# Attention and a quantised residual block on one core: q's first transfers on three queues, a cast ahead of a square, and a copy into another buffer

## The chip, the cores and the metric

The kernel runs on one core of a Trainium2 chip. The time is device time of one launch in microseconds. The core has five engines with instruction streams of their own: PE (TensorE, matrix products), DVE (VectorE), ACT (ScalarE), POOL (GpSimd) and SP (SyncE, used here only to issue DMA transfers). A transfer is issued by one of SP, ACT and POOL, in the order of that engine's own instructions, and the bytes are moved by DMA engines that all of them use. "PEclk" in the profile is the TensorE clock that was granted, as a share of full speed.

## The reference

Input x has shape (4, 128, 64, 64) in fp32. Two layers follow each other. The first is a group norm, attention with 4 heads of 32 channels over the 4096 positions of each image, a projection, and x added again. The second is a residual block of two 3x3 convolutions with weights quantised to three bits, each with a batch norm over the batch and all positions.

```python
# first layer
xn = group_norm(x)                     # 8 groups of 16 channels
q, k, v = split(einsum('oc,bchw->bohw', qkv_w, xn) + qkv_b)
attn = softmax(einsum('bhid,bhjd->bhij', q, k) * d ** -0.5)
x = x + einsum('oc,bchw->bohw', proj_w, einsum('bhij,bhjd->bhid', attn, v)) + proj_b
# second layer
residual = x
out = relu(batchnorm(conv3x3(x, lsq_quantize(w1)), gamma1, beta1))
out = batchnorm(conv3x3(out, lsq_quantize(w2)), gamma2, beta2)
x = relu(out + residual)
```

## The kernel before

Channels lie on the 128 partitions. The order of all instructions is written by hand: functions emit parts of the work, and a schedule calls them, so each engine executes its instructions in the order in which the Python code emitted them. Where two instructions of different engines touch the same buffer, the framework puts in a wait.

**Attention** takes most of the time. There are 32 blocks (4 images, 8 blocks of 512 queries), each against 32 tiles of 128 keys. `scores` multiplies k by q (L447, tile `s`, the name `s_0_1` below means key tile 0, group 1) and ACT takes the exponential (L449, `p`). `weights` multiplies p by v (L461). Sums of p go to DVE (L476) and to accumulating transfers of POOL. fp32 operands are held as two parts, hi and lo, both in the type fp32r of the matmuls; hi is written by ACT, and lo (the value less hi) by DVE. Projections of later blocks are side work between the scores.

**The start.** Chunks of x are loaded by SP and ACT, statistics and the norm are computed, and `project_parts` makes k, q and v of the first blocks: PE writes `pk`, `pq` and `pv` (L322), `parts` writes hi (L356, ACT) and lo (L357, DVE) into `kst` and `qst`, and these are sent to where the scores read them. For most blocks this goes by DRAM, one transfer of 512 KB out (`kd`, `qd`, L361) and smaller ones back in. For the very first block alone, `direct` (L393 to L409) moves k and q within the on-chip memory: 8 transfers of 64 KB for k (L407), then 8 of 128 KB for q (L409). The first four of each are for g=0 (heads 0 and 1), the next four for g=1 (heads 2 and 3). They go by turns to `nc.sync` and `nc.gpsimd`. SP's next instruction after its four of q is the store `kd` of the second block; POOL's next are two small loads `al`. The scores of a key tile are four matmuls for each g, and the first key tile's g=0 scores read all four transfers of q for g=0.

**The convolutions.** In each layer of the residual block the output is made in 16 bands of 16 rows (1024 positions, two psum banks of 512). Most bands (2 to 14, in the second convolution without 8) are made "by two": two output rows are computed together from sums and differences of input rows, with fewer matmuls. For them `mixed_parts` makes the sums `vo` and `vi` on DVE (L600 to L603), ACT casts them to hi (`uo`, `ui`, L605), and DVE makes lo (`lo`, `li`, L609). `conv_by_two` (L870) issues 24 matmuls into four banks: a0, a1 (inner products), c0, c1 (outer rows). `rows_of_two` then makes the two output rows:

- `copy` (L884, ACT) copies a1 from psum to the odd rows of the result `cv`;
- `inner` (L887 and L889, DVE) writes a0 + a1 to the even rows and a0 − a1 to the odd rows of `cv`, with sums for the batch norm. L889 overwrites in place what L884 wrote and L887 reads;
- `outer` (L894, ACT, twice) copies c0 and c1 into the rows of a buffer `co`, then an accumulating transfer of POOL (L896) adds `co` to `cv`. For bands 13 and 14, `outer_at_once` (L900, DVE) adds c0 and c1 to `cv` directly.

When a band is complete in `cv`, ACT squares it with a running sum (L1011, its output goes to `co` as a place to discard it). This waits for the band's accumulating transfer, so squares are put off: they stand in a list `behind`, and `flush(1)` issues all but the newest. In the loop of `layer`, a band's instructions are emitted in this order: `copy`; in the first convolution `flush(1)`; `begin` (the first part of a later band's preparation: sums and casts); `flush(1)`; `inner`; `rest` (lo of that later band); `later` (loads); `outer`.

Band 15 is the last and is computed in the ordinary way: ACT casts its input tile t to `hi` (L619, in `begin`), DVE makes `lo` (L622, in `rest`), and after the loop PE computes it as `c_last` (L837) in two halves, in banks that band 13's c0 and c1 had before. Batch norm statistics of `c_last` are taken by DVE (L1041), and the batch norm ends the layer.

Of the kernel before, what the change touches and what calls it, by code (L numbers as in the profile page):

```python
# [18 lines left out]
ALU = mybir.AluOpType  # L19
# [8 lines left out]
FB = 512  # L28
# [50 lines left out]
def _fast_body(ctx, tc, x, norm_w, norm_b, qkv_wt, qkv_b, proj_wt, proj_b,  # L79
               w1, alpha1, gamma1, beta1, w2, alpha2, gamma2, beta2, out, cnt):  # L80
    nc = tc.nc
    B, C, H, W = x.shape
# [146 lines left out]
    def stack_tile(name):  # L229
        return kpool.tile([P, KW], F32R, name=name, tag="k")  # L230

    def f32(t):
        return t.bitcast(F32)
# [154 lines left out]
    def k_tile(b, j):  # L388
        ks[b, j] = stack_tile(f"k{b}_{j}")[:, : 2 * FB].rearrange("p (g n) -> p g n", n=FB)
        return ks[b, j]  # L390

    def q_tile(b, j):
        qs[b, j] = qpool.tile([P, 2, 2, FB], F32R, name=f"q{b}_{j}", tag="q")  # L393
        return qs[b, j]

    def direct(what, t):

        u = k_tile(0, 0) if what == "k" else q_tile(0, 0)
        engines = nc.sync, nc.gpsimd
        for g in range(2):  # L400
            for c, s in enumerate((0, 2, 1, 3)):
                i, part = divmod(s, 2)
                h = 2 * g + i
                src = t[h * D : (h + 1) * D, :, :]
                eng = engines[(4 * g + c) % len(engines)]
                if what == "k":
                    eng.dma_start(out=f32(u)[s * D : (s + 1) * D, g, :], in_=src[:, part, :])  # L407
                else:
                    eng.dma_start(out=f32(u)[s * D : (s + 1) * D, g, :, :], in_=src)  # L409
# [420 lines left out]
    def conv(parts, ps, j, w):  # L830
        hi, lo = parts
        r0 = j * RB
        n = 0
        for part in (hi, lo):
            for tap in range(TAPS):
                kh, kw = divmod(tap, 3)
                nc.tensor.matmul(ps.rearrange("p (r w) -> p r w", w=W), w[:, tap, :],  # L837
                                 part[:, r0 + kh : r0 + kh + RB, kw : kw + W],
                                 start=(n == 0), stop=(n == 2 * TAPS - 1))
                n += 1  # L840

    def conv_tile(i, b, g):
        return pss.tile([P, 2, FB], F32, name=f"c{i}_{b}_{g}", tag="s")
# [19 lines left out]
    def conv_by_two(parts, a, c, i):  # L863

        for m, ps, w in ((1, a[0], wmix[:, 0, :, :]), (2, a[1], wmix[:, 1, :, :]),
                         (0, c[0], wq[i][:, 0:3, :]), (3, c[1], wmix[:, 2, :, :])):
            n = 0
            for part in parts:
                for kw in range(3):
                    nc.tensor.matmul(ps.rearrange("p (r w) -> p r w", w=W), w[:, kw, :],  # L870
                                     part[m][:, :, kw : kw + W], start=(n == 0), stop=(n == 5))
                    n += 1

    def rows_of_two(a, c, y, sums, name, at_once):

        def of(t, e):
            return t.rearrange("p (r e w) -> p r e w", e=2, w=W)[:, :, e, :]

        even, odd = of(y, 0), of(y, 1)
        a0, a1, c0, c1 = (u.rearrange("p (r w) -> p r w", w=W) for u in (*a, *c))  # L880
        outer_rows = f32(stack_tile(f"co{name}"))[:, : 2 * FB]

        def copy():
            nc.scalar.copy(odd, a1)  # L884

        def inner():
            nc.vector.scalar_tensor_tensor(even, odd, 1.0, a0, ALU.mult, ALU.add,  # L887
                                           accum_out=sums[:, 0:1])
            nc.vector.scalar_tensor_tensor(odd, odd, -1.0, a0, ALU.mult, ALU.add,  # L889
                                           accum_out=sums[:, 1:2])  # L890

        def outer():
            for e, u in enumerate((c0, c1)):
                nc.scalar.activation(of(outer_rows, e), u, AF.Identity,  # L894
                                     accum_out=sums[:, 2 + e : 3 + e])
            nc.gpsimd.dma_start(out=y, in_=outer_rows, accum_op=ALU.add)  # L896

        def outer_at_once():
            for e, u, v in ((0, even, c0), (1, odd, c1)):
                nc.vector.scalar_tensor_tensor(u, u, 1.0, v, ALU.mult, ALU.add,  # L900
                                               accum_out=sums[:, e : e + 1])

        return copy, inner, outer_at_once if at_once else outer, outer_rows
# [26 lines left out]
    def layer(i, prepare, start=None):  # L930
# [17 lines left out]
        def flush(left=0):  # L948
            while len(behind) > left:
                behind.pop(0)()  # L950

        def stats(m, j, ps):
            if m in on_act:
                return
            nc.vector.bn_stats(st[:, 2 * plain.index(m) + j, :], ps[:, j, :])

        def keep(m, j, ps):
            b, g = bandlist[m]
            c = 2 * g + j
            if m not in on_act:  # L960
                nc.scalar.copy(cv[b][:, c * FB : (c + 1) * FB], ps[:, j, :])
                return
            k = two.index(m)
            nc.scalar.activation(cv[b][:, c * FB : (c + 1) * FB], ps[:, j, :], AF.Identity,
                                 accum_out=sums[:, 4 * k + j : 4 * k + j + 1])
            if j == 1:
                junk = f32(stack_tile(f"co{i}_{m}"))[:, : 2 * FB]
                nc.scalar.activation(junk, cv[b][:, 2 * g * FB : (2 * g + 2) * FB], AF.Square,
                                     bias=shift[:, 1:2], accum_out=squares[:, k : k + 1])

        def origin():
            mv = small.tile([P, 2], F32, name=f"first{i}", tag="mv")
            nc.vector.bn_aggr(mv, st[:, 0:2, :].rearrange("p j s -> p (j s)"))
            nc.vector.tensor_copy(shift[:, 0:1], mv[:, 0:1])
            nc.vector.tensor_scalar(shift[:, 1:2], mv[:, 0:1], -1.0, None, ALU.mult)

        def banks(m):
            b, g = bandlist[m]
            a = conv_tile(i, b, g)
            if (len(two) - 1 - two.index(m)) % 2:  # L980
                c = [psa.tile([P, FB], F32, name=f"c{i}_{b}_{g}{j}", tag="a") for j in "xy"]
            else:
                c = pss.tile([P, 2, FB], F32, name=f"c{i}_{b}_{g}z", tag="s")
                c = [c[:, j, :] for j in range(2)]
            return [a[:, j, :] for j in range(2)], c

        done = start(banks, stats, keep, origin) if start else {}
        for m, (b, g) in enumerate(bandlist[:-1]):
            if m in done and m not in BY_TWO[i]:
                continue  # L990
            begin, rest, later = prepare(m)
            if m in BY_TWO[i]:
                if m in done:
                    a, c = done[m]
                else:
                    a, c = banks(m)
                    conv_by_two(ready[i, b, g], a, c, i)
                y = cv[b][:, 2 * g * FB : (2 * g + 2) * FB]
                k = two.index(m)
                copy, inner, outer, junk = rows_of_two(a, c, y, sums[:, 4 * k : 4 * k + 4], f"{i}_{m}",  # L1000
                                                       m > 12)
                copy()
                if i == 0:
                    flush(1)
                begin()
                flush(1)
                inner()
                rest()
                later()
                outer()  # L1010
                behind.append(lambda y=y, k=k, junk=junk: nc.scalar.activation(  # L1011
                    junk, y, AF.Square, bias=shift[:, 1:2], accum_out=squares[:, k : k + 1]))
                continue
            ps = conv_tile(i, b, g)
            for j in range(2):
                conv(ready[i, b, g], ps[:, j, :], j, wq[i])
            begin()
            flush(1)
            rest()
            later()  # L1020
            for j in range(2):
                stats(m, j, ps)
                keep(m, j, ps)
            if m == 0:
                origin()
# [68 lines left out]
    def opening(banks, stats, keep, origin):  # L1094
# [35 lines left out]
        return {0: None, 1: None, 2: done}  # L1130

    a1, c1 = layer(0, first, opening)
    nc.vector.tensor_copy(cnt, pools["bad"][0:1, 0:1])

# [42 lines left out]
    def second(m):  # L1177
# [10 lines left out]
        return begin, rest, later  # L1188

    a2, c2 = layer(1, second)  # L1190
    for b in (B - 2, B - 1):
        for i in range(4):
# [470 lines left out]
```

## Time and profile before

| what | value |
|---|---|
| time, median of 3 runs | 2470.35 us (2469.05 to 2471.85) |
| profiled execution, its own time | 2469.57 us |
| span of the profiled execution | 2467.9 us |
| mean granted TensorE clock | 0.994 |
| L449 ACT exponentials | 1951.3 us, 2048 of 1033 ns |
| L447 PE scores | 1137.3 us, 8192 |
| L461 PE products with v | 1025.8 us, 16384 |
| L870 PE products by two | 150 for each of uo, ui, lo and li, some 43.9 us each |
| L1011 ACT squares | 28.8 us, 25 of 1152 ns |

The page gives one execution. Each group's first number is its busy time, "xN" the number of instructions, and what follows the bar is how long the engine had stood idle just before them and whom it waited for. Busy time of DVE and ACT is within a tenth of that of PE over the whole, so the page's sums alone do not tell which of them an edit has to reach; the chain of waits and PE's gaps do.

The convolutions lie at the end: the first from about 2250 to 2332 us, the second to 2437, and after it the last additions and stores to 2468. In the table of busy tenths the last slices show it:

```profile
PE   9999999999999999999999999999999999999995
DVE  6899888989998888899989888898999999999897
ACT  5999888999988899999998899999999999996686
DMA  6887677678776766688767676678666666766627
```

### The profile page before, as it was taken

To read this page: it belongs to the slowest core of one execution; us is meant where nothing else is said; L and a number is where in the kernel's file an instruction comes from. 1 tells how busy PE (TensorE), PEld (TensorE's weight loads), DVE (VectorE), ACT (ScalarE), POOL (GpSimd) and SP (SyncE) were. 2 spreads that over 40 slices of the span, in tenths; PEclk is the share of its full clock that TensorE was granted. 3 is DMA by queue.
4 is the path that set the end of the run, shared out by engine and by line. 5 is a ranking of instruction groups with operands and counts; after the bars stand their busy time and mean duration, and the time that the engine had idled before them with its cause. 6 is when DMAs were issued, how large, how long until landed. Compare 5 with 4: busy or idle time off the path is not lost.

```text
span 2467.9 us, 65119 instructions
## 1 busy us (share of the span) xinstructions
PE 2432.5 (99%) x28396; PEld 1445.7 (59%) x28396; DVE 2197.6 (89%) x1560; ACT 2182.4 (88%) x2446; POOL 300.3 (12%) x527
## 2 busy tenths in 40 slices
PE   9999999999999999999999999999999999999995
PEld 6555555555555555555555555555555555557774
DVE  6899888989998888899989888898999999999897
ACT  5999888999988899999998899999999999996686
POOL 1111111111101111111101111111010100111110
PEclk9999999999999999999999999999999999999997
DMA  6887677678776766688767676678666666766627
GB/s 195 191 191 167 172 176 176 167 187 210 169 164 167 181 161 163 145 205 205 172 151 175 173 175 156 156 190 204 149 141 147 149 138 144 160 150 167 162 56 236
DMA packets 128389, 416.21 MB, mean 169 GB/s; under 512 B 33808, under 2 KB 34960, under 8 KB 99424
## 3 DMA queue, kind: packets, MB, share of 16 engines
q0 software_dynamic: 48688, 292.38, 52.3%
q1 hardware_dynamic: 78832, 118.54, 17.1%
q8 instruction: 225, 3.69, 0.6%
q10 hardware_dynamic: 576, 1.05, 0.1%
q14 instruction: 68, 0.56, 0.1%
HBM read 107.75 MB, written 56.43 MB: 67 GB/s over the span
## 4 chain that ended last, share of the span: by engine, by line
PE 93%; DVE 3%; DMA 2%; issue 1%; ACT 0%; SPq 0%; POOL 0%; POOLq 0%; ACTq 0%; DVEq 0%
PE s L447 43%; PE acc L461 39%; PE c L837 2%; PE c L870 1%; DMA rm<-p 1%; PE pk L322 1%; PE l L493 1%; PE pq L322 1%; PE pv L322 1%; PE po L322 1%; PE c_last L837 1%; DVE res L1201 1%; DVE li L609 0%; DVE lo L609 0%; DMA cv<-co 0%
## 5 line engine op out<-in xcount | busy, mean ns | idle before, releaser
L449 ACT ACTIVATE p<-s 128x1024 f32<-128x1024 f32 x2048 | 1951.3, 1033 | 197.3 <-PE s L447 153.1
L476 DVE TENSOR_TENSOR r<-r,p 128x2048 f32<-128x2048 f32 x768 | 1757.9, 2289 | 63.1 <-ACT p L449 12.0
L447 PE MATMUL s<-q,k 64*128 64x512 f32 x8192 | 1137.3, 409 | 1.9 <-issue 1.7
L461 PE MATMUL acc<-p,v 128*32 128x256 f32 x16384 | 1025.8, 383 | 0.0
L447 PEld LDWEIGHTS s<-q,k 64*128 64x128 f32 x8192 | 716.1, 184 | 408.3 <-issue 166.2
L461 PEld LDWEIGHTS acc<-p,v 128*32 128x32 f32 x16384 | 462.7, 109 | 483.1 <-issue 248.1
L471 POOL DMA_DIRECT2D rm<-p x160 | 140.4, 877 | 780.3 <-ACT p L449 658.2
L357 DVE SCALAR_TENSOR_TENSOR kst<-pk,b,kst 128x512 fp32r<-128x512 f32 x32 | 24.0, 751 | 80.5 <-PE s L447 61.7
L474 DVE TENSOR_TENSOR r<-p,p 128x2048 f32<-128x2048 f32 x32 | 73.2, 2287 | 8.3 <-ACT p L449 7.0
L357 DVE SCALAR_TENSOR_TENSOR qst<-pq,b,qst 128x512 fp32r<-128x512 f32 x32 | 24.0, 750 | 59.2 <-PE s L447 46.5
L361 POOL DMA_DIRECT2D qd<-qst x31 | 23.0, 742 | 267.1 <-DVE qst L357 217.7
L497 POOL DMA_DIRECT2D r<-rm x32 | 27.2, 851 | 224.6 <-PE s L447 81.2
L870 PE MATMUL c<-ui,wmix 128*128 128x512 f32 x150 | 43.9, 400 | 0.0
L870 PE MATMUL c<-li,wmix 128*128 128x512 f32 x150 | 43.8, 400 | 0.0
L361 POOL DMA_DIRECT2D kd<-kst x27 | 20.0, 741 | 177.3 <-DVE kst L357 162.1
L605 ACT CAST uo<-vo 128x1024 fp32r<-128x1024 f32 x25 | 26.3, 1054 | 16.0 <-DVE vo L600 15.0
L469 POOL DMA_DIRECT2D rm<-p x32 | 17.8, 558 | 175.2 <-ACT p L449 106.9
L1011 ACT ACTIVATE co<-cv,shift 128x1024 f32<-128x1024 f32 x25 | 28.8, 1152 | 11.1 <-DMA cv<-co 11.1
L493 PE MATMUL l<-r,ones 128*32 128x256 f32 x512 | 37.7, 379 | 0.0
L538 POOL DMA_DIRECT2D y<-x x32 | 21.0, 657 | 121.6 <-DVE x L537 112.8
L356 ACT ACTIVATE kst<-pk,b 128x512 fp32r<-128x512 f32 x32 | 22.4, 700 | 14.5 <-PE pk L322 14.5
L322 PE MATMUL po<-av,wp 128*32 128x512 f32 x256 | 33.4, 593 | 0.4 <-DVE av L527 0.4
(268 smaller groups left out, 1220.2 us busy)
## 6 DMA issues: line engine op xcount, KB each, us to landing
rm<-p POOLq DMA_DIRECT2D x192, 1024.0 KB, 7.7
r<-rm POOLq DMA_DIRECT2D x32, 1024.0 KB, 7.6
q<-qd SPq DMA_DIRECT2D x248, 128.0 KB, 4.5
x<-in_x_dram SPq DMA_DIRECT2D x86, 256.0 KB, 6.2
k<-kd SPq DMA_DIRECT2D x124, 128.0 KB, 4.8
qd<-qst POOLq DMA_DIRECT2D x31, 512.0 KB, 5.0
kd<-kst POOLq DMA_DIRECT2D x27, 512.0 KB, 4.4
cv<-co POOLq DMA_DIRECT2D x21, 512.0 KB, 4.8
```

The lines of the kernel that those rows point to most:

```text
L322: nc.tensor.matmul(out[cs, :], w[:, cs], x, start=True, stop=True)
L357: nc.vector.scalar_tensor_tensor(lo, ps[what], bias, t[:, 0, :], ALU.add, ALU.subtract)
L361: (nc.sync if start else nc.gpsimd).dma_start(out=dst[b, j].rearrange("s p n -> p s n"), in_=t)
L447: nc.tensor.matmul(s[:, i, :], k[r, half, c0 : c0 + P], q[r, half, part, :], start=(part == 0), stop=(part == 1))
L449: nc.scalar.activation(pts[step][:, 2 * half : 2 * half + 2, :], s, AF.Exp, scale=SCALE)
L461: nc.tensor.matmul(acc[n][h * D : (h + 1) * D, cs], v[:, kt % KB, h * D : (h + 1) * D], pt[:, h, cs], start=(kt == 0 and half == 0), stop= ...
L471: nc.gpsimd.dma_start(out=msum[n], in_=pt, accum_op=ALU.add)
L474: nc.vector.tensor_tensor(rsum[n], pts[step - 1], pt, ALU.add)
L476: nc.vector.tensor_tensor(rsum[n], rsum[n], pt, ALU.add)
L493: nc.tensor.matmul(t["l"][h * D : (h + 1) * D, cs], ones, r[:, h, cs], start=first, stop=end)
L837: nc.tensor.matmul(ps.rearrange("p (r w) -> p r w", w=W), w[:, tap, :], part[:, r0 + kh : r0 + kh + RB, kw : kw + W], start=(n == 0), stop ...
L870: nc.tensor.matmul(ps.rearrange("p (r w) -> p r w", w=W), w[:, kw, :], part[m][:, :, kw : kw + W], start=(n == 0), stop=(n == 5))
```

## The change

There are three edits.

In `direct`, q's eight transfers go to SP, POOL, ACT and POOL in turn, where they went to SP and POOL by turns. SP issues two, POOL four, ACT two. ACT's two stand in its program after its own write of `qst` (L356) and before those of the next blocks' `kst`, and the first of them waits for DVE's lo of q. k's transfers stay as they were.

In the loop of `layer`, the first `flush(1)` of the first convolution is left out for bands 13 and 14. At band 13, the cast of band 15 (L619), in `begin`, then comes before the square of band 11, which the second `flush(1)` issues. At band 14 nothing lies between the two flushes.

In `rows_of_two`, `copy` writes into the first half of the band's `co` buffer, in one piece (`copied`), instead of the odd rows of `cv`. `inner` reads it there. L889 so no longer overwrites what L887 reads. `outer` writes into the same buffer and so now has to wait until `inner` has read it. The `co` buffer is taken at `copy`, earlier in the order of buffers than before, and `co` shares its pool of tiles with `vo`, `vi`, k and the input tiles. Two lines are added, so that what follows L882 is two lines further down.

```diff
@@ -396,7 +396,7 @@
     def direct(what, t):
 
         u = k_tile(0, 0) if what == "k" else q_tile(0, 0)
-        engines = nc.sync, nc.gpsimd
+        engines = (nc.sync, nc.gpsimd) if what == "k" else (nc.sync, nc.gpsimd, nc.scalar, nc.gpsimd)
         for g in range(2):
             for c, s in enumerate((0, 2, 1, 3)):
                 i, part = divmod(s, 2)
@@ -880,13 +880,15 @@
         a0, a1, c0, c1 = (u.rearrange("p (r w) -> p r w", w=W) for u in (*a, *c))
         outer_rows = f32(stack_tile(f"co{name}"))[:, : 2 * FB]
 
+        copied = outer_rows[:, :FB].rearrange("p (r w) -> p r w", w=W)
+
         def copy():
-            nc.scalar.copy(odd, a1)
+            nc.scalar.copy(copied, a1)
 
         def inner():
-            nc.vector.scalar_tensor_tensor(even, odd, 1.0, a0, ALU.mult, ALU.add,
+            nc.vector.scalar_tensor_tensor(even, copied, 1.0, a0, ALU.mult, ALU.add,
                                            accum_out=sums[:, 0:1])
-            nc.vector.scalar_tensor_tensor(odd, odd, -1.0, a0, ALU.mult, ALU.add,
+            nc.vector.scalar_tensor_tensor(odd, copied, -1.0, a0, ALU.mult, ALU.add,
                                            accum_out=sums[:, 1:2])
 
         def outer():
@@ -1000,7 +1002,7 @@
                 copy, inner, outer, junk = rows_of_two(a, c, y, sums[:, 4 * k : 4 * k + 4], f"{i}_{m}",
                                                        m > 12)
                 copy()
-                if i == 0:
+                if i == 0 and m < 13:
                     flush(1)
                 begin()
                 flush(1)
```

## The prediction

> **What bounds the kernel now.** I read the page's busy table first, then the chain that ended last, then the chain between 12 and 50 us (where the first edit lies), the windows and the queues of that stretch, and last the timelines of the end of the first convolution (where the other two lie).
>
> ```profile
> span 2467.9 us, 65119 instructions
> ...
> PE 2432.5 (99%) x28396; PEld 1445.7 (59%) x28396; DVE 2197.6 (89%) x1560; ACT 2182.4 (88%) x2446; POOL 300.3 (12%) x527
> ...
> PE 93%; DVE 3%; DMA 2%; issue 1%; ACT 0%; SPq 0%; POOL 0%; POOLq 0%; ACTq 0%; DVEq 0%
> ```
>
> TensorE is busy for 2432.5 of 2467.9 us. Whatever shortens DVE or ACT counts only where PE waits for it, so the whole question is which of PE's few gaps the edits touch. The first lies at the start:
>
> ```profile
> 22.24 0.87 PE pv L322 x32
> 23.11 1.72 issue
> 24.84 3.28 PE s L447 x12
> 28.12 2.29 PE pv L322 x64
> 30.41 1.59 PE s L447 x9
> ...
> 34.29 1.59 PE s L447 x12
> ```
>
> PE ends its projections at 23.11 and begins the first scores at 24.84. Those 12 score matmuls take 3.28 us, where a later dozen takes 1.59; the 64 pv matmuls take 2.29, where two groups of 32 at 0.87 make 1.74. Between 23.11 and 30.41 so 7.30 us pass for 3.33 us of work: 3.97 us lost. The windows and SP's queue say why (columns of the windows: us, busy time of PE, PEld, DVE, ACT and POOL, granted clock, DMA share, GB/s):
>
> ```profile
> 19.00:21.00 2.00, 2.00 (x68) 1.66 (x64) 1.51 (x3) 0.95 (x2) 2.00 (x5) 1.00 1.00 238
> 21.00:23.10 2.10, 2.10 (x64) 1.50 (x52) 1.42 (x3) 0.95 (x2) 0.15 (x1) 1.00 0.83 242
> 23.10:24.84 1.74, 0.02 (x4) 0.03 (x1) 1.28 (x2) 0.00 (x0) 0.00 (x0) 1.00 0.92 265
> 24.84:28.12 3.28, 3.28 (x16) 2.15 (x20) 0.00 (x0) 1.84 (x2) 0.00 (x0) 0.60 0.34 108
> ```
> ```profile
> 18.23 3.40 SPq L409 DMA_DIRECT2D q<-qst  x4
> 21.72 1.84 SPq L361 DMA_DIRECT2D kd<-kst  x1
> ```
> ```profile
> 18.09 1.94 POOL L409 DMA_DIRECT2D q<-qst  x4
> ```
>
> q (8 transfers of 128 KB, the first four for heads 0 and 1, g=0, the rest for g=1) is issued from 18.09 to 21.63, four by POOL and four by SP; the DMA engines are meanwhile 83 to 100% busy. By the DMA records the last of g=0 lands at 24.75 (SP's second), and PE starts 0.09 later; the last of g=1 lands at 25.56 (SP's fourth), and PE begins g=1 at 25.75. The clock is half from 25.5 to 28.9.
>
> The second gap is at the end of the first convolution:
>
> ```profile
> 2313.64 0.58 ACT L884 COPY cv<-c 128x512 f32<-128x512 f32 x1
> 2317.01 1.15 ACT L1011 ACTIVATE co<-cv,shift 128x1024 f32<-128x1024 f32 x1 [2.78 <-DMA cv<-co]
> ...
> 2318.16 1.17 ACT L619 CAST hi<-t 128x1188 fp32r<-128x1188 f32 x1
> ```
> ```profile
> 2319.36 1.40 DVE L622 TENSOR_TENSOR lo<-t,hi 128x1188 fp32r<-128x1188 f32 x1 [2.91 <-ACT hi L619]
> 2320.67 0.68 DVE L900 SCALAR_TENSOR_TENSOR cv<-cv,c_1x 128x512 f32<-128x512 f32 x1
> ```
> ```profile
> 2321.51 2.39 PE L837 MATMUL c_last<-hi,wq 128*128 128x512 f32 x9 [0.65 <-DVE cv L900]
> ```
>
> ACT stands for 2.78 us at square 11 (L1011), which waits for band 11's accumulating DMA, and band 15's cast stands behind it. So lo (DVE), L900 behind lo, and PE's c_last, which takes the bank that L900 reads, are all late: PE waits 0.65 us.
>
> **What the Trainium skill says.** DMA: Bandwidth & Descriptors, section Issuing engines are not separate DMA queues: transfers of all issuing engines share the same 16 DMA engines, and more issuers save only sequencer time. The trace agrees as far as it goes: share 1.00 at 238 GB/s from 19 to 21 with two issuers. The same page, Queues, rings and completion order, says that a DMA engine takes turns between the queues it has work for; no row here shows the turns, but by it a third queue would give q a larger share against others. TensorE: Matmul & The Clock Gate, Part 1: The HAM clock gate, says that the array is halved after an idle window of about 3.4 us, and that windows run freely. The trace fits: half for 3.4 us (25.5 to 28.9) after a stretch of 3.4 us that held the 1.72 us gap.
>
> **Part 1, q by three queues.** SP issues two of q instead of four, POOL four as before, ACT two. Per group the order is SP, POOL, ACT, POOL. Issues: SP's four q took 0.54, 0.59, 1.55 and 0.59 us. In the new order SP's are done at about 18.23+0.54+0.59=19.4, 2.3 us earlier. ACT's are free after qst (15.68+0.69=16.37, but it waits for DVE's lo at 17.15); ACT issued x at 0.46 each at the start, so at 17.15 to 18.1; above, if a busy ring holds it as SP's third was held, 1.55 each, to 20.3. POOL's fourth stays at 19.54+0.49=20.03. So the last issue moves from 21.63 to 20.0.
>
> That gain is not the landing's gain. From 20.4 (k's last landing) to 25.56, 5.2 us, at about 240 GB/s 1.24 MB were moved; q itself is 1.05 MB. Taking its 1.05 MB from 20.4 at that rate gives 24.8, estimated, for the last of q if nothing else moved. And something else comes in: SP's next instruction is the store kd (L361, 512 KB, 2.1 us at that rate). It reaches SP at 19.4 instead of 21.72, and its data (kst_1's lo) are there about then. Full weight on it gives 26.9, half 25.8. Full weight on it gives 26.9, half 25.8. But a queue's bytes move in the order of issue: kd stands behind q on SP's own queue, and meets only the last of POOL's and ACT's. I take a small share, 24.9 for the last of q. g=0 is earlier for certain: its second SP transfer (24.75) becomes ACT's first, issued by 17.2 to 18.7 instead of 18.81; POOL's second landed at 23.76, so scores begin at 23.9.
>
> Gain: four score matmuls of g=0 take 1.59/3=0.53 and end at 24.4; g=1 follows its data at 25.0 instead of 25.75. As the landing alone is sure, I count 25.56−24.9=0.66: −0.66. The half clock I leave in place: in the 3.41 us before 25.51 PE was busy for 1.01 (22.10 to 23.11) and 0.67 (24.84 to 25.51), 49%; now 1.01+0.53+0.5=2.04, 60%, and no row shows from which share the clock stays. If it stays, another 3.41/2=1.7 goes. Bounds: −3.97 (gap and half clock both gone; no more is lost there) and +1.3 (last of q at 26.9, on kd's full weight).
>
> Against it: ACT's two issues stand before its cast of kst_1 (17.10 to 17.79), which PE's banks wait for. At 0.46 each the cast slips to 18.1, 1.0 late; ACT then has 1.05 of idle before each next cast, and is on time again after one. DVE's lo for k takes 0.75 and its v 0.68, 1.43 in a period of 1.73, so 0.3 per period is made good: in the four periods to 24 us the lag is all but gone. If the issues take 1.55, the cast slips 2.5 and PE stands some 1 to 2 us before 23.1; that is idle time moved from 23.1 to 19, since scores wait for q anyhow. Cost 0, bound +0.5.
>
> **Part 2, the cast ahead of the square.** flush at that place is left out for m=13 (and 14, whose begin does nothing). ACT has copied by 2314.22, t of band 15 has been loaded, so hi runs 2314.2 to 2315.4, lo behind it on DVE. DVE has inner of 12 from 2315.03 to 2316.45; lo after it, or between, ends by about 2317.9, L900's pair by 2319.3. PE's own queue is free at 2319.99+0.87=2320.86. So c_last starts at 2320.86: −0.65, the whole gap. Square 11 then begins after hi, at 2317.0 still (its DMA sets it), so squares are not later. What is late next: the last c_last ends at 2330.37 and batch norm follows its statistics; squares end at 2326.4 and their reduction at 2327.3, before the bn_stats of c_last's second half. That cover is 3.1 us, reduced to 2.5. The 0.65 passes on. Bounds 0 (t late) and −0.65.
>
> **Part 3, `copied`.** L884 writes a contiguous half of `co` instead of every second row of `cv`. Same 128x512: 0.58. The second inner (L889) no longer waits for the first. In the trace L887 starts at 2286.98 and L889 at 2287.70, 0.72 apart; L900's pair without such a wait is 0.61 apart (2320.67, 2321.28). So DVE saves 0.11 per band, 25 bands 2.75 us. DVE works ahead of PE here: PE is busy 10.00 of every 10 us from 2250 to 2320, so 2.75 us come to nothing in time. Price: outer's ACTIVATE (L894) overwrites `copied` and so waits for L889. In the first convolution ACT started outer at 2288.05, and L889 ends at 2288.39: 0.34 wait, in 11 or 12 bands. A band lasts 5.71 us of PE (24 matmuls at 0.238); ACT is busy 4.75 to 4.9 of it, so 0.8 idle covers 0.34. In the second, inner ends first (2371.3 against outer's 2373.4): no wait. The `co` buffer is claimed at the copy instead of at outer, and loads of t for bands 10 to 15 wait for a DVE instruction 1 to 2 us later than before; they have about 4 us in hand. Cost 0; bounds −0.3 and +1.
>
> **Sum.** −0.66−0.65+0=−1.3. Against the profiled execution (2469.57, of which 2467.9 is span and 1.7 around it) that is 2468.3; the median shown is 0.78 above it, 2470.35−1.3=2469.0.
>
> **Rivals.** (a) The start mended: the clock is not halved, −1.3−1.7=−3.0, 2467.3; with q in by 23.5 as well, −3.97−0.65=−4.6, 2465.7. For it: 1.7 us of idle in a window of 3.4 is all that halved it. Against: 1.05 MB at 240 GB/s. (b) Bound by the DMA engines: g=0's end moves not at all, because kd and q share as before: −0.65, 2469.7. For it: share 0.83 to 1.00. Against: ACT's queue is empty when its first q comes. (c) Slower: ACT becomes the bound of the first convolution, since outer waits behind inner and all that follows on ACT (the copy that frees PE's banks, the casts) with it. It decides from a wait of 5.71−4.75=0.96 per band. If DVE runs inner a band's operation (1.22) later than in the trace, the wait is 0.34+1.22=1.56, 0.6 over, times 11 bands: +6.6−1.3=+5.3, 2475.7. For it: DVE's own lead over PE falls to 0.57 us by band 14. Against: an earlier pair, 0.11 each. (d) The start gets worse, kd taking q's place: +1.3−0.65=+0.65, 2471.0.
>
> **How the numbers follow.** Chances: forecast 0.42, (a) 0.28, (b) 0.11, (c) 0.12, (d) 0.07. A change of 0.2% is 4.9 us, about what a measurement of this kernel tells from no change. Forecast, (b) and (d) lie within it. Of (a) the full form, −4.6, falls just short of it, and the three runs before differ by 2.8 us; so I put 0.16 of (a)'s 0.28 beyond: faster 0.16. Slower is (c), 0.12. The same is the rest, 0.42+0.12+0.11+0.07=0.72. The range leaves out (c) and a little of (a)'s far end: 2465.2 to 2471.5.
>
> **What would show it.** Right: scores begin near 23.9, the last of q lands near 24.9, the clock still dips; L619 stands before L1011 at the end of the first convolution and the 0.65 gap is gone; L889 starts 0.61 after L887; ACT idle before L894 about 0.3; PE's sum from 2250 to 2320 unchanged. Wrong: PEclk 1.00 throughout the start (then a), last landing of q past 25.6 (then b or d), PE gaps named to ACT between 2260 and 2315 (then c).

## The result, and the profile after

| | before | changed |
|---|---|---|
| median | 2470.68 us (2468.42 to 2473.38, 22 runs) | 2467.48 us (2466.29 to 2469.01, 22 runs) |
| ratio | | 0.9987, 95% interval 0.9981 to 0.9993 |
| profiled execution: time, span | 2469.57, 2467.9 us | 2467.72, 2466.0 us |

The changed kernel takes 3.2 us less by the medians; the interval says 1.7 to 4.7. A second comparison further down gave 2.25 by the medians.

The busy table of the page hardly moves, as the kernel is still bound by TensorE:

```profile
span 2466.0 us, 65112 instructions
...
PE 2432.2 (99%) x28396; PEld 1444.9 (59%) x28396; DVE 2196.3 (89%) x1560; ACT 2183.3 (89%) x2446; POOL 300.2 (12%) x527
```

**The start.** The chain of waits of the changed kernel (start, length, what; all in us):

```profile
18.59 5.26 DMA q<-qst
23.85 0.04 issue
23.89 0.97 PE s L447 x4
24.86 0.16 issue
25.02 0.46 PE s L447
25.48 0.02 issue
25.50 1.17 PE s L447 x7
26.67 1.88 PE pv L322 x64
28.55 1.60 PE s L447 x12
```

Scores begin at 23.89 instead of 24.84 (9.83 us after PE's first projection `pk` instead of 11.16; the inputs of this execution came 0.38 later), and a transfer of q, issued by SP at 18.59, still decides it. Four matmuls of g=0 take 0.97 us where 0.53 is their length, then the dozen waits for g=1. So the landing of q remains the limit; it is earlier, not gone. The windows of the same stretch, columns as before:

```profile
19.00:21.00 2.00, 1.89 (x52) 1.24 (x44) 1.39 (x3) 1.19 (x3) 2.00 (x5) 1.00 0.85 243
21.00:23.10 2.10, 2.09 (x60) 1.74 (x64) 2.10 (x4) 0.72 (x2) 0.54 (x1) 1.00 1.02 290
23.10:24.84 1.74, 1.68 (x32) 0.94 (x24) 1.46 (x3) 0.61 (x1) 0.00 (x0) 1.00 0.95 274
24.84:28.12 3.28, 3.10 (x65) 2.43 (x68) 0.63 (x2) 2.90 (x3) 0.00 (x0) 1.00 0.27 92
```

The granted clock is 1.00 where before it was 0.60, and the transfers move 274 and 290 GB/s where they moved 265 and 242. PE is busy 1.89 of 2.00 us from 19 to 21: ACT's two issues (0.60 and 0.63) push its cast of kst back, and PE waits a little for it, as the bound of the prediction allowed.

**The end of the first convolution.** ACT's timeline, then lines of DVE's and of PE's:

```profile
2311.55 0.59 ACT L886 COPY co<-c 128x512 f32<-128x512 f32 x1
2312.01 1.21 ACT L619 CAST hi<-t 128x1188 fp32r<-128x1188 f32 x1
2315.90 1.15 ACT L1013 ACTIVATE co<-cv,shift 128x1024 f32<-128x1024 f32 x1 [2.68 <-DMA cv<-co]
```
```profile
2313.68 1.39 DVE L622 TENSOR_TENSOR lo<-t,hi 128x1188 fp32r<-128x1188 f32 x1
2314.99 0.68 DVE L902 SCALAR_TENSOR_TENSOR cv<-cv,c_1x 128x512 f32<-128x512 f32 x1
```
```profile
2318.62 0.87 PE L870 MATMUL c_2z<-lo,wmix 128*128 128x512 f32 x3
2319.34 2.31 PE L837 MATMUL c_last<-hi,wq 128*128 128x512 f32 x9
```

The cast stands behind ACT's copy, the square waits for its transfer after it, DVE's L902 (the old L900) begins 4.3 us before PE needs the bank, and PE goes into c_last without a gap.

**The copied products.** DVE's timeline of the kernel before, then of the changed kernel, then ACT's:

```profile
2286.98 0.68 DVE L887 SCALAR_TENSOR_TENSOR cv<-cv,c 128x512 f32<-128x512 f32 x1
...
2287.70 0.69 DVE L889 SCALAR_TENSOR_TENSOR cv<-cv,c 128x512 f32<-128x512 f32 x1
```
```profile
2308.98 0.68 DVE L889 SCALAR_TENSOR_TENSOR cv<-co,c 128x512 f32<-128x512 f32 x1
...
2309.58 0.68 DVE L891 SCALAR_TENSOR_TENSOR cv<-co,c 128x512 f32<-128x512 f32 x1
```
```profile
2310.39 0.60 ACT L896 ACTIVATE co<-c_0z 128x512 f32<-128x512 f32 x1 [0.18 <-DVE cv L891]
```

The pair starts 0.60 us apart, where it was 0.72, and outer (L896, the old L894) waits 0.18 us for inner. From 2250 to 2320 PE is busy 10.00 of every 10 us, as before.

### The profile page after: what moved, and what is told of

Same layout as the page of the kernel before. It is cut to its first block, busy times and chain, and to the rows that moved or that the text cites. A ratio compares the mean times of both kernels' runs of the same rounds, so it can differ in the third digit from the quotient of the medians.

```text
span 2466.0 us, 65112 instructions
## 1 busy us (share of the span) xinstructions
PE 2432.2 (99%) x28396; PEld 1444.9 (59%) x28396; DVE 2196.3 (89%) x1560; ACT 2183.3 (89%) x2446; POOL 300.2 (12%) x527
## 4 chain that ended last, share of the span: by engine, by line
PE 96%; DMA 2%; DVE 1%; issue 0%; ACT 0%; SPq 0%; POOL 0%; ACTq 0%; POOLq 0%; DVEq 0%
PE s L447 43%; PE acc L461 39%; PE c L870 3%; PE c L837 2%; DMA rm<-p 1%; PE l L493 1%; PE po L322 1%; PE pq L322 1%; PE pk L322 1%; PE pv L322 1%; PE c_2z L870 1%; PE c_last L837 1%; DVE res L1203 1%; PE c_0z L870 0%; PE c_1x L870 0%
## 5 line engine op out<-in xcount | busy, mean ns | idle before, releaser
L356 ACT ACTIVATE kst<-pk,b 128x512 fp32r<-128x512 f32 x32 | 22.3, 700 | 15.3 <-PE pk L322 13.2
```

## The experiments

Two measures serve below. One is the stretch from PE's first projection pk to the 64 pv matmuls behind the first dozen of scores, which leaves out how late an execution's inputs came: 14.37 us in the profile of before (28.05−13.68), 12.54 in that of the changed kernel (26.60−14.06). The other is the mean granted clock, listed for every execution to three places. A dip of 3.4 us to half speed takes 3.4·0.5/2467=0.0007 from it; before's profiled execution has 0.994 and the changed kernel's 0.995. The sign is rough, since it is rounded and a dip elsewhere counts too. In every trace the clock is also half for the last 23 to 27 us, where PE has nothing left to do, and that length alone can move the mean by as much as a dip. Held against the 14 traces, the sign errs once: three of the four with a dip have 0.994, the fourth (the changed kernel with inner late, further down) and the ten without have 0.995. So the counts of executions at 0.994 are estimates of how often the clock dips.

### One edit at a time

First edit alone (q's queues; the other two as before):

```diff
-        engines = nc.sync, nc.gpsimd
+        engines = (nc.sync, nc.gpsimd) if what == "k" else (nc.sync, nc.gpsimd, nc.scalar, nc.gpsimd)
```

> Only the first edit: q's first transfers by SP, POOL and ACT. Theory (the clock at the start is the main part): first scores near 23.9 us, last of q near 25.2, PEclk 1.00 from 23.1 to 30.4, and 2.2 to 2.5 us less than before. Rival (the landing alone counts, the clock is chance): the clock is half again in some executions, and 0.7 us less. Rival (the copied buffer carries the gain): under 1 us less here.

Second edit alone:

```diff
-                if i == 0:
+                if i == 0 and m < 13:
                     flush(1)
```

> Only the second edit: band 15's cast ahead of the square. Theory: PE's gap of 0.65 us before c_last is gone, L619 begins when ACT's copy of band 13 ends, and the time is 0.65 us less. Rival (the next wait takes it): the gap before c_last is gone but the wait at the end of the first convolution grows by as much, and the time is that of before.

Third edit alone:

```diff
-            nc.scalar.copy(odd, a1)
+            nc.scalar.copy(copied, a1)
...
-            nc.vector.scalar_tensor_tensor(odd, odd, -1.0, a0, ALU.mult, ALU.add,
+            nc.vector.scalar_tensor_tensor(odd, copied, -1.0, a0, ALU.mult, ALU.add,
```

> Only the third edit: inner products copied to the buffer of outer rows. Theory: DVE's pair of L889 and L891 starts 0.61 us apart instead of 0.72, PE is busy 10.00 of every 10 us from 2250 to 2320 as before, ACT waits some 0.3 to 0.4 us a band before outer, and the time is unchanged within 0.3 us. Rival (DVE's lead matters): 1 us or more less. Rival (ACT's new wait matters): 1 us or more longer, with PE gaps named to ACT.

| kernel | median | executions at 0.994 | ratio |
|---|---|---|---|
| before, beside them | 2469.72 us | 16 of 41 | |
| q's queues alone | 2468.37 us | 0 of 13 | 0.9997 (0.9988 to 1.0005) |
| cast alone | 2469.11 us | 8 of 13 | 0.9997 (0.9989 to 1.0006) |
| copied alone | 2469.76 us | 6 of 13 | 0.9999 (0.9991 to 1.0008) |

No single ratio is clear of 1. The times say more once executions with the same sign are compared, as 0.994 and 0.995 differ by more than the edits do. Among those at 0.995, the mean is 0.75 us below before's for the queues (13 executions against 25 of before), 0.82 for the cast (5) and 0.03 for the copy (7); among those at 0.994, 0.72 for the cast (8 against 16) and 0.01 for the copy (6). The 95% intervals reach 0.5 to 0.8 us to each side, so the gains of the queues and of the cast are clear of zero, the cast's barely, and the copy shows none.

The traces agree. The queues: pk to pv is 12.48 us, the clock stays full, and the median is 1.35 lower, less than the 2.2 expected. The cast: the gap before c_last is gone, and the median is 0.6 lower. Copied: the gap before c_last is still there (0.86), and the median is before's within 0.1.

What had not been expected is in the windows of the cast-alone kernel, whose start is that of before:

```profile
23.10:24.84 1.74, 0.13 (x8) 0.00 (x0) 1.35 (x2) 0.01 (x1) 0.00 (x0) 1.00 0.91 268
24.84:28.12 3.28, 3.16 (x44) 2.28 (x48) 0.00 (x0) 2.23 (x3) 0.00 (x0) 1.00 0.31 107
```

PE stands idle here as in before, 1.70 us, and the clock is 1.00 all the same. The copied-alone kernel shows this too (gap 1.74, clock 1.00). So the half clock in the profile of before was one execution's lot.

The traces show part of what this lot hangs on. Between two changes of the granted clock there lies in every trace a whole number of steps of 3.413 us (in before 6, 1 and 707 of them), and the steps lie differently against the program in each execution. In before the gap, 23.12 to 24.84, lies inside one step (22.10 to 25.51), and the next step is at half. In the cast-alone and copied-alone kernels it runs over the end of a step (at 24.83 and 24.92), so that two steps share it, and the clock stays full. This is not the whole rule: in the kernel before with inner late (further down) the gap, 23.44 to 25.14, also lies inside one step (22.27 to 25.69), and the clock stays full.

The start without a dip can now be measured. In these two kernels pk to pv takes 13.44 and 13.46 us: that, and not 14.37, is what the old start takes.

### Is it the idle stretch that brings the dip?

Small idle matmuls were put on PE between its last projection and the first scores of the kernel before:

```diff
             load_k(0, j + 1)
+    keep_warm(12)
```

> The kernel before, with 12 small matmuls on PE (1.5 us at full clock) between the last projection and the first scores, where PE stood idle for 1.72 us; q's transfers and all else as before. Theory (the idle stretch halved the clock, and that cost 1.7 us besides the wait): scores still begin near 24.8 us, PEclk stays 1.00 from 24.84 to 30.41, the first dozen takes near 2 us instead of 3.28, and the time is 1.5 to 1.9 us less. Rival (only the landing of q counts): the time is that of before. Rival (the clock falls whatever PE does there): PEclk 0.6 again.

Each of the 12 stands twice in the trace, so that they took 2.88 us instead of 1.5 and pushed the scores to 26.07. The time was 2469.52 (0.9999, 0.9991 to 1.0008), and not 1.5 to 1.9 less, with 1 of 13 executions at 0.994. With half as many:

> The kernel before, with 6 calls of the idle matmul (each stands twice in the trace, 0.12 us each, 1.44 us together) in PE's gap before the first scores, so that they end before q's data are there. Theory (the half clock is a matter of chance with that gap, in some 16 of 41 executions, and costs some 1.2 us each time): nearly no execution has a mean clock of 0.994, scores begin near 24.9 us, and the time is 0.5 us less than before, at that of the executions of before that ran at 0.995 (2468.9). Rival (the gap has nothing to do with the clock): a third or more of the executions at 0.994.

PE's timeline of that kernel:

```profile
23.20 1.60 PE L315 MATMUL idle<-gavg 128*128 128x128 f32 x12
24.95 2.25 PE L447 MATMUL s<-q,k 64*128 64x512 f32 x12
```

Now the idle matmuls end before q lands, scores begin at 24.95 as in before, and none of 13 executions is at 0.994, against 8 of 33 of before beside them. The mean is 2469.18 against 2469.55, 0.37 less (0.5 expected; medians 2469.49 and 2469.60, ratio 0.9999, 0.9991 to 1.0007). The time alone shows nothing. The counts agree with the theory: of the two kernels with idle matmuls 1 of 26 executions is at 0.994, and of before beside them 24 of 74.

Over all comparisons that list clocks, before was at 0.994 or below in 53 of 133 executions, with a mean of 2470.73 us, and above in 80, with 2469.18: 1.55 us apart. Kernels with the new queues and no other change to the convolutions' order were at 0.994 in 4 of 103.

### The changed kernel again

> The changed kernel once more, beside the others of this call. Theory (0.9 us from q's landing, 0.65 from the cast, 0.5 on the mean from the clock, none from the copied buffer): 2.0 to 2.1 us less than before, at most a few executions at 0.994. Rival (the three edits help each other): 3.2 us less, as in the first comparison.

2467.35 against 2469.60, ratio 0.9990 (0.9982 to 0.9999); 1 of 13 at 0.994. The means differ by 2.04. The sum of the parts fits this: 13.43 (mean of three kernels with the old start, no dip) less 12.67 (mean of five with the new) is 0.76 for q's landing; 0.81 for the cast, the mean gap before c_last in five traces without that edit (0.6 to 1.0; a sixth, of the kernel with 12 idle calls, has 1.6); (0.40−0.04)·1.55=0.56 for the clock; 2.1 together. Among executions at 0.995 alone, where the clock hardly enters, the changed kernel's mean is 1.78 below before's, against 0.76+0.81=1.57. The 2.1 lies within the first comparison's interval (1.7 to 4.7), but the further 1.1 us of its 3.2 stay open: how often before dipped there isn't listed, and its mean, 2470.74, is that of the executions at 0.994 elsewhere. In two comparisons more it dipped in 16 of 26 and 13 of 33, so this share moves from set to set.

### What sets q's landing?

The store kd (512 KB) was suspected. Three kernels tried to take it away from q.

> The changed kernel, with the second block's store kd (512 KB) issued by POOL after its q and its two small loads, near 21.5 us, instead of by SP near 20.4, so that it stands behind all of q on POOL's queue. Theory (kd shares the DMA engines with the last of q): the last of q lands by 24.9 instead of 25.4, the first dozen of scores ends 0.4 us earlier, and the time is 0.3 to 0.5 us less than the changed kernel's. Rival (q's own 1.05 MB sets its landing): no difference. Rival (the later k waits for kd): longer by up to 1 us, with a PE gap named to k.

> The changed kernel, with the second block's store kd (512 KB) issued by ACT after its third write of kst, near 21.6 us, and the load of k that reads it moved behind it, so that kd starts after all of q. In the trace of the run with kd on POOL the store was still issued at 20.39, so that run did not move it in time. Theory (kd takes bytes from the last of q): the last of q lands 0.4 us or more earlier, measured from PE's first projection (11.5 us after it in the changed kernel), the first dozen of scores ends as much earlier, and the time is 0.4 us less than the changed kernel's 2467.4. Rival (q's own bytes set its landing): the last of q again 11.5 us after PE's first projection, and the same time.

In neither did it come late: it was issued at 20.39 and 20.12, against 20.39. Their medians, 2467.22 and 2467.04, tell nothing of it, but their traces do. On POOL, behind all of POOL's q, kd left the landing as it was: the last of q came 11.48 us after pk (11.31 and 11.53 in the two profiles of the changed kernel). The other kernel did the opposite of what was meant. ACT issued kd as early as before, and SP, free of it, issued the next block's store already at 21.37:

```profile
20.12 0.39 ACTq L363 DMA_DIRECT2D kd<-kst  x1
```
```profile
21.37 0.40 SPq L363 DMA_DIRECT2D kd<-kst  x1
```
```profile
24.28 2.86 PE L453 MATMUL s<-q,k 64*128 64x512 f32 x12 [0.73 <-DMA q<-qst]
27.07 1.96 PE L323 MATMUL pv<-wn,xh 128*32 128x128 f32 x64
```

By the DMA records 626 KB of stores moved there before q's last byte, where it is 284 to 392 KB in the six other traces with q on three queues. The last of q landed 12.07 us after pk, and pk to pv took 13.30 (27.07−13.77), against 12.48 to 12.89. So stores can take time from q, in this one trace some 0.6 us.

The third held all stores of the start until ACT's last kst:

```diff
+                if start:
+                    held.append(store)
...
+        if (what, j) == ("k", 4):
+            for n in range(1, 5):
+                held[n - 1](nc.scalar if n == 1 else nc.sync)
+                if n < 4:
+                    load_k(0, n)
```

> The changed kernel, with the stores kd of the next blocks of k held until ACT has written the last kst of the start: the first of them is issued by ACT near 23.7 us, the others and the loads of k behind it by SP in the old order. In the two earlier tries the store was issued at 20.4 and 20.1, so they did not test this. Theory (kd takes bytes from the last of q): the last of q lands near 11.0 us after PE's first projection or earlier (11.3 to 11.5 in the changed kernel), the first dozen of scores ends 12.3 us or less after it (12.6 to 13.0), and the time is 0.4 us less. Rival (q's own bytes set its landing): the same landing within 0.2 us and the same time. Rival (the next blocks' k comes too late): PE gaps named to k, and longer by 0.5 us or more.

ACT's timeline, and the windows:

```profile
22.91 0.39 ACTq L363 DMA_DIRECT2D kd<-kst  x1
```
```profile
19.00:21.00 2.00, 1.86 (x56) 1.20 (x51) 1.56 (x3) 1.22 (x3) 2.00 (x5) 1.00 0.97 280
21.00:23.10 2.10, 2.10 (x68) 1.76 (x64) 2.10 (x4) 0.70 (x2) 0.34 (x1) 1.00 1.02 273
```

kd now comes 9.0 us after pk instead of 6.3. Its first bytes move when 24 KB of q are left, where it was 172 and 216 KB in the two profiles of the changed kernel. Yet the last of q lands 11.40 us after pk (25.27−13.87), between their 11.31 and 11.53. So the one store that meets q in the changed kernel does not measurably hold it up, and the theory falls for it, while nearly twice the store traffic did hold q up. What is left as the limit is q's own transfers; no run changes how many bytes they carry. The time, 2466.95 (0.9988 of before, 0.9981 to 0.9994), is the lowest median of all, but 0.4 below the changed kernel in another comparison is not a difference that these runs resolve.

The last kernel asks from the other side: one queue for all of q.

```diff
-        engines = nc.sync, nc.gpsimd
+        engines = (nc.sync, nc.gpsimd) if what == "k" else (nc.sync,)
```

> The kernel before, with all eight of q's first transfers issued by SP. Theory (the issue of SP is slow, 0.6 us with stalls of 1.5, and the idle stretch of PE halves the clock by chance, the oftener the longer it is): the last issue is near 25 us, the last of q lands 1.5 us or more after before's, PE's gap before the scores is 2.5 us or more, and over half of the executions, instead of some 40 of 100, have a mean clock of 0.994; together 1.5 to 3 us more than before. Rival (the DMA engines alone set q's landing): the landing and the time are those of before. Rival (the clock's dip has nothing to do with the gap): no more executions at 0.994 than before.

Its windows:

```profile
12.00:17.00 5.00, 5.00 (x48) 4.47 (x51) 1.16 (x6) 0.24 (x1) 0.55 (x1) 0.68 0.05 4
...
21.00:23.10 2.10, 2.10 (x72) 1.76 (x64) 1.46 (x3) 1.05 (x2) 0.14 (x1) 1.00 0.72 199
23.10:24.84 1.74, 1.74 (x57) 1.35 (x48) 1.35 (x2) 0.69 (x2) 0.00 (x0) 1.00 0.78 210
24.84:28.12 3.28, 1.85 (x14) 0.66 (x5) 1.35 (x2) 0.91 (x2) 0.00 (x0) 1.00 0.80 210
28.12:30.41 2.29, 2.26 (x27) 1.54 (x31) 0.00 (x0) 1.74 (x3) 0.00 (x0) 0.66 0.36 122
```

The theory missed the size, and on the clock the rival's forecast came (6 of 13 executions at 0.994 against 13 of 33), though the gap did not grow longer as the theory needs. The median is 2470.02 (0.9999 of before, 0.9991 to 1.0007). In the profiled execution the last of q lands 12.40 us after pk (28.02−15.62) against 11.88 in before; but the four of g=0 come first in the one queue, so that scores begin at 10.39 after pk against 11.16, and PE's idle time is cut up into pieces of 0.95, 0.20 and 0.20. The clock dips twice there, once from 11.8 to 15.2 us, before q is issued and behind 1.59 us of idle PE (0.95 at that place in before). The windows give a cleaner reading: the transfers moved 199 to 210 GB/s from one queue, 238 and 242 from two (before, 19 to 23.1), 280 and 273 from three with kd late. From one queue the issuing sets this: SP issued the first six of q at one each 0.62 us, and 128 KB in 0.62 us are 210 GB/s. From two queues it does not, as all of q was issued by 21.63 and bytes were due until 25.1; there the DMA share was 0.83 from 21 to 23.1, and 1.02 with three queues.

### What would the slower rival have cost?

Inner was emitted after rest, first in the changed kernel, then in the kernel before:

```diff
-                inner()
                 rest()
+                inner()
```

> The changed kernel, with inner emitted after rest: DVE makes lo and li of the later band (1.22 us each) before the inner products. Outer on ACT, which waits for inner because it overwrites the copied products, comes 2.4 us later, while lo and li are earlier. It prices the forecast's slower rival. That rival as put (ACT becomes the bound from a wait of 0.96 us per band): a wait of about 2.6 us before outer in each of the first convolution's bands, some 1.6 over ACT's spare time, PE gaps of that size named to ACT, and 15 to 20 us more. Other theory (the wait eats the lead of the casts first, and DVE's order is as full as before): ACT's wait grows by 2 us or less a band, and the time rises by less than 5 us.

> The kernel before, with inner emitted after rest, as in the run that priced the slower rival (2483.4 us), but with the products still copied to cv, so that outer need not wait for inner. It tells what of the 13.8 us there came from the new wait. Theory (ACT, queued behind outer's wait, casts late for the band after, and DVE's inner, which frees PE's banks, is late behind those casts): here ACT does not wait before outer, PE has no gaps of over 0.2 us in the first convolution but that before c_last, and the time is within 2 us of before. Rival (inner itself comes too late for PE's banks): gaps of 1.6 us named to DVE again, and 10 us or more over before.

In the changed kernel: 2483.39 us (1.0058 of before, 1.0042 to 1.0073). In the kernel before: 2478.54 (1.0034, 1.0021 to 1.0047). ACT's timeline of the first, two bands in a row, and PE's:

```profile
2287.57 0.60 ACT L896 ACTIVATE co<-c_3x 128x512 f32<-128x512 f32 x1 [2.78 <-DVE cv L891]
...
2295.12 0.60 ACT L896 ACTIVATE co<-c_0z 128x512 f32<-128x512 f32 x1 [2.78 <-DVE cv L891]
```
```profile
2295.15 0.95 PE L870 MATMUL c<-ui,wmix 128*128 128x512 f32 x3 [1.59 <-DVE cv L891]
```

A band takes 7.55 us (2295.12−2287.57) instead of 5.71, 1.84 more, with a wait of 2.78 on ACT: 2.78−1.84=0.94 was covered. The rival's point of decision, 0.96, fits this. PE's gaps are named to DVE and not to ACT, though, since the bank that PE waits for is freed by inner, which is behind casts that ACT made late. In the kernel before, outer never waits for inner, yet PE loses time too:

```profile
2329.04 3.67 PE L837 MATMUL c_last<-hi,wq 128*128 128x512 f32 x9 [3.96 <-DVE cv L900]
```

Here inner itself is late for the banks (3.2 us in two gaps in the bands), and DVE is late for c_last. So the theory there fell by its size: by the means the order alone costs 8.9 us (7.9 by the medians), not 2. Against the changed kernel's 2467.4 the same move costs 16.0. That some 7 us come with the new wait is likely but no clean split, as the two kernels differ in the other edits too: the 3.96 before c_last is 0.5 in all with the cast ahead, while PE's gaps named to inner are seven with 9.6 us together instead of two with 3.2. All five executions of the kernel before with inner late are at 0.994, and the profiled one has half clock after the gap of 3.96:

```profile
2330.00:2334.00 4.00, 4.00 (x13) 3.12 (x12) 2.98 (x16) 3.23 (x6) 0.00 (x0) 0.61 0.14 56
```

## Why the prediction came out as it did

The direction and the range (2465.2 to 2471.5) held, but the range was wide enough to hold no change at all. The size, −1.3, was too small: 3.2 and 2.25 were measured. Step by step:

- **Scores and q's landing**: 23.9 forecast, 23.89 in the profile. That it fits to 0.01 is luck: after pk 10.2 us were forecast, and 9.83 and 10.43 came in the two profiles. The last of q was put at 24.9, which is 11.2 after pk; it came at 11.31 and 11.53. The gain of 0.66 was 0.76. But its working held two errors, which offset each other. kd was given 0.1 us, which is 24 KB at the rate used, where 284 to 392 KB of it moved before q's last byte; and the rate was taken as the same 240 GB/s, where three queues moved some 280 from 21 us on.
- **The half clock, left in place**: this step failed. It was the forecast's largest error. The profile showed the dip, and it was taken as part of before's time; then the choice seemed to be between keeping it and losing it. By the mean clock, before has it in some 40 of 100 executions, and the kernels with the new queues in 4 of 103. Its removal is worth 0.56 on the mean, neither 0 nor the 1.7 of rival (a). The sign named for (a), full clock through the start, came, and the first median even meets (a)'s 2467.3; but the second comparison and the sum of the parts say some 2 us and not 3.0. What the median of 22 runs does then depends on the share in that set.
- **ACT's issues ahead of the cast of kst**: cost 0 held. The cast came 1.4 us later (18.89 against 17.10, pk 0.38 later itself) and PE lost 0.12 us from 19 to 23.1, while the data for the scores were not there yet.
- **The cast ahead of the square**: the whole gap went, 0.65 as forecast from before's profile, and 0.81 on the mean of five traces.
- **`copied`**: 0 held, with DVE's saving (0.12 a band) and ACT's wait (2.29 at the first band, where ACT had little to do, then 0.15 to 0.19 in eight bands, where 0.34 was taken) both hidden behind PE.
- **The rivals**: (b), bound by the DMA engines, was half true: PE still waits for q, but the rate rose with the queues and g=0's landing moved. (c) stayed away, as outer's wait is 0.2 us a band and not 0.96. (d), kd in q's place, did not happen in the changed kernel; with a second store beside kd it did, by some 0.6 us.

The Trainium skill's page TensorE: Matmul & The Clock Gate, Part 1: The HAM clock gate, says that windows run freely and warns that the count of cold matmuls differs from run to run. The prediction cited the first half and used the single profile as if the second were not there; 53 of 133 executions at 0.994 bear it out. Nor did the trace fit the page as well as the prediction said: the page has the clock halved after an idle window, and by the prediction's own count PE was busy for 49% of the one before the dip.

## What to carry to other kernels

A dip of the clock behind a short idle stretch of PE is a matter of chance: before it is priced, look how often it occurs, in the clocks of many executions or in the traces of kernels that share the stretch. Measure stretches between two events of one engine, not times since the start, when changes of a microsecond are compared, and compare the times of executions with the same clock. And an instruction that has to wait for another engine can do so at no cost within the spare time of its own engine per round: here some 0.9 us a band, so that a wait of 0.2 cost nothing and one of 2.78 cost 1.84.

## What the runs showed of the hardware

- PE idle for some 1.7 us before the first scores was followed by half clock in one of four traces (before; not cast alone, copied alone, nor before with inner late) and, by a mean clock of 0.994, in some 40 of 100 executions; with idle matmuls in the gap 1 of 26 is at 0.994. After 3.96 us idle the one trace has it, and all five executions are at 0.994. Seven gaps of 1.2 to 1.6 us, one a band, were followed by none (changed kernel with inner late).
- Each dip seen in the traces (five, in four kernels) lasted 3.41 us, and all changes of the clock within a trace are whole multiples of 3.413 us apart.
- Transfers at the start, most of them within the on-chip memory, moved 199 to 210 GB/s with q issued from one queue (there as fast as SP issued), 228 to 240 from two (six traces, means from 19 to 23.1 us), and 267 to 286 from three (seven traces), with the same bytes of q. The Trainium skill's page DMA: Bandwidth & Descriptors, section Issuing engines are not separate DMA queues, says that more issuers only save the sequencer's time. From one queue to two that fits; from two to three the rate rose although issuing was not what held q up, and the DMA share from 21 to 23.1 us was 0.80 to 0.86 with two queues and 0.98 to 1.02 with three.
